# Rational layer: numerators of a couple in one PSUM tile, and another split of the ratio between VectorE and GpSimd

## The chip, the cores and the metric

The kernel runs on one core of a Trainium2 chip. The metric is the device time of one launch in microseconds (us); lower is better. Engines are named as in the profile: PE is TensorE, DVE VectorE, ACT ScalarE, POOL GpSimd, SP the queue that issues most DMAs.

## The reference

Four layers run one after the other on x of shape (8, 16, 128, 128). Each normalises x in groups (2 channels to a group), computes a convolution-like function of it, and adds the result to x. Layer 0 is a small attention block over 3x3 patches, layer 1 a gated 1x1 convolution, layer 2 the rational convolution that the change touches, layer 3 a spline convolution. Layer 2 is:

```python
def _L2_conv_ref(x, A, Bc):
    K, DEG_P, DEG_Q = 3, 6, 4
    B, C, H, W = x.shape
    xp = jnp.pad(x, ((0, 0), (0, 0), (1, 1), (1, 1)))
    wins = jnp.stack([xp[:, :, i:i + H, j:j + W] for i in range(K) for j in range(K)])
    pw = wins[..., None] ** jnp.arange(DEG_P, dtype=x.dtype)
    P = jnp.einsum('pbchwi,fcpi->fpbchw', pw, A)
    Q = 1.0 + jnp.abs(jnp.einsum('pbchwi,fcpi->fpbchw', pw[..., 1:1 + DEG_Q], Bc))
    out = jnp.sum(P / Q, axis=(1, 3))
    return jnp.transpose(out, (1, 0, 2, 3))
```

For each of the 9 positions of the window, each input channel c and each output channel f there is one polynomial P of degree 5 and one denominator Q = 1 + |polynomial of degree 4|. The ratios are summed over the positions and the input channels. So 9 x 16 x 16 ratios are made for each of 8 x 128 x 128 pixels, and their number sets the work.

## The kernel before

All of x stays in SBUF, as 128 partitions (8 images x 16 channels) by 16384 pixels. In layer 2 a helper `powers` (line 929) makes x to x^5 of two image rows and sends them to DRAM; `turn` (line 955) loads ten rows of them, with halo, into four of eight tiles `f`, where 32 partitions hold the powers of four channels. The profile shows all 64 calls of `powers` at work between 3546 and 3893 us, near the layer's start, while the first couples run.

The layer's unit of work is a **couple** (class at line 981): for 8 rows from `r0`, a half `g` of the images, a half `k` of the rows (4 rows, 512 pixels), a window position `n`, and two images out of four (`i`). There are 16 x 2 x 2 x 9 x 2 = 1152 couples. A couple has two halves `ab`, one for each image, and each half is a PSUM tile of 128 partitions by 2 banks of 512 columns: 4 channels to a 32-row strip of TensorE, 16 outputs to a channel, so that 256 (channel, output) pairs fill 128 partitions twice. The steps of a couple are:

- `product` (line 966): four matmuls of 32 rows by 64 columns for the denominators `pd` (weights `wb`), four more for the numerators `pn` (weights `wa`), for each half. In the profile an f32 matmul is two records, so a half of `pd` or `pn` is 8 records.
- `absolute` (line 989), ACT: t = |pd|, 1024 columns for each half, into the SBUF tile `t` (4 buffers).
- `ln` and `exp` (lines 994 and 999), ACT, through the helper at line 152: u = ln(1 + t), then u = exp(-u), a first estimate of 1/Q; 2048 columns each, in the SBUF tile `u` (4 buffers).
- `step` (line 1002), DVE: t = (t + 1) u, which is Q times the estimate.
- `times` (line 1008), DVE, one for each half: u = pn u, the ratio before correction.
- The ratio corrected by one Newton step is u (2 - t). It is made in two ways. For the first bank of each half, `ratio` (line 1014, DVE) forms (t - 2) u. For the second bank, `correction` (line 1021, POOL) forms v = t u, and TensorE adds 2 u - v. `correction` waits until the next couple's step has ended (line 1025).
- `over_channels` (line 1046), PE: the sums over 4 channels by matmuls with the constant `gather`, into the accumulators `acc0` and `acc1`, in three parts: part 0 the finished ratios with weight -1, part 1 u with weight 2, part 2 v with weight -1. It serves two couples at a time, 4 matmuls of 512 columns to a part. After the last position the accumulator is added to x, and the statistics for layer 3 are taken (lines 1067 and 1068).

The order on ACT and on DVE is written out by hand: `in_turn` (line 210) ties each instruction of an engine to the one named before it. On PE only the sums are tied, behind the last product issued; the products follow the order in which they are written and what they wait for. The main loop (line 1087) runs over couples `m`; `before` is couple m-1, `then` m+1. Within a turn ACT does absolute(m, half 1), ln(m), absolute(m+1, half 0), exp(m), and DVE does times(m-1, half 1), ratio(m-1), step(m), times(m, half 0). `products` (line 1030) interleaves the numerators of one couple's half with the denominators of another's, matmul by matmul. PSUM has 8 banks: `pd` takes one buffer of 2, `pn` two buffers of 2, and the accumulators 2.

Of the kernel before, what the change touches and what calls it, by code (L numbers as in the profile page):

```python
# [9 lines left out]
F32 = mybir.dt.float32  # L10
AF = mybir.ActivationFunctionType
ALU = mybir.AluOpType
# [5 lines left out]
BC = B * C  # L18
HW = H * W
HP, WP = H + 2, W + 2  # L20
NCH = HW // 512
# [79 lines left out]
def kernel(  # L101
# [20 lines left out]
    nc = tc.nc  # L122
    mm = nc.tensor.matmul
# [3 lines left out]
    cpool = ctx.enter_context(tc.tile_pool(name="const", bufs=1))  # L127
# [15 lines left out]
    order = mybir.DependencyInfo(mybir.DependencyClass.NoSync, mybir.DependencyReason.DATA)  # L143
# [66 lines left out]
    def in_turn(engine, ins):  # L210

        if engine in chain:
            tc.add_manual_dep(ins, chain[engine].name, order, reason="in turn")
        chain[engine] = ins
        return ins
# [3 lines left out]
    for n in range(5):  # L219
        t = cpool.tile([BC, BC], F32, name=f"w1_{n}")  # L220
        nc.gpsimd.memset(t, 0.0)
        for b in range(B):
            r = slice(b * C, (b + 1) * C)
# [7 lines left out]
    bn1 = cpool.tile([BC, NCH, 6], F32, name="bn1")  # L231
    top = cpool.tile([BC, NCH], F32, name="top")
    x1d = dram.tile([BC, HW], F32, name="x1d")
    with ExitStack() as l0:
        wp = l0.enter_context(tc.tile_pool(name="w0", bufs=1))
        with tc.tile_pool(name="x0", bufs=2) as xp:
            bn0 = xp.tile([BC, NCH, 6], F32, name="bn0", bufs=1)
            for j in range(8):
                t = xp.tile([BC, HW // 8], F32, name="xj")
# [3 lines left out]
            mean0, _, rs0, d0 = group_stats(bn0, "0")  # L243
        lo, hi = _WHERE["center"][1], _WHERE["last"][2]
# [24 lines left out]
        for a in range(2):  # L269
            src = aff_d[:, a : a + 1].rearrange("(d p g c) a -> p g c (d a)", p=2, g=2, c=C)  # L270
            for odd in range(2):
                for g in range(2):
                    for i in range(3):
                        r = 64 * (g ^ odd) + 16 * i
# [489 lines left out]
    with ExitStack() as l1:  # L764
# [93 lines left out]
        class Chunk:  # L858
# [10 lines left out]
            def product(self, p, w):  # L869
                for i in range(2):  # L870
                    cols = bass.ts(i, 512)
                    in_turn("pe1", mm(p[:, cols], w, self.y[:, cols], start=True, stop=True).ins)
# [37 lines left out]
                    getattr(chunks[i], do)()  # L910


    bn3 = cpool.tile([BC, NCH, 6], F32, name="bn3")
    with ExitStack() as l2:
        wp = l2.enter_context(tc.tile_pool(name="w2", bufs=1))
        tmp = l2.enter_context(tc.tile_pool(name="tmp2", bufs=1))
# [49 lines left out]
        def product(p, w, g, k, n, q):  # L966

            dh, dw = divmod(n, 3)
            for u in range(4):
# [6 lines left out]
                    stop=True,  # L976
                ).ins

        class Couple:
            def __init__(self, r0, g, k, n, i):
                self.r0, self.g, self.k, self.n, self.i = r0, g, k, n, i
                self.pd, self.pn = {}, {}

            def at(self, ab):
                return self.g, self.k, self.n, 2 * self.i + ab

            def absolute(self, ab):
                if ab == 0:  # L990
                    self.t = tmp.tile([128, 2, 2, 512], F32, name="t", bufs=4)
                in_turn("act", nc.scalar.activation(self.t[:, ab], self.pd.pop(ab), AF.Abs).ins)  # L992

            def ln(self):

# [9 lines left out]
                ).ins  # L1005
                self.stepped = in_turn("dve", ins)

            def times(self, ab):
                ins = nc.vector.tensor_mul(self.u[:, ab], self.pn.pop(ab), self.u[:, ab]).ins  # L1009
                in_turn("dve", ins)  # L1010

            def ratio(self):
                r = self.u[:, :, 0]
                ins = nc.vector.scalar_tensor_tensor(  # L1016
                    r, self.t[:, :, 0], 2.0, r, op0=ALU.subtract, op1=ALU.mult
                ).ins
                in_turn("dve", ins)

            def correction(self, behind):

                self.v = tmp.tile([128, 2, 512], F32, name="v", bufs=3)
                ins = nc.gpsimd.tensor_mul(self.v, self.t[:, :, 1], self.u[:, :, 1]).ins  # L1024
                tc.add_manual_dep(ins, behind.name, apart, reason="shared port")

        apart = mybir.DependencyInfo(mybir.DependencyClass.Sync, mybir.DependencyReason.DATA)
        last = {}

        def products(num, ab, den):  # L1030


            todo = []
            if den:
                den.pd[1 - ab] = ps.tile([128, 2, 512], F32, name="pd")
                todo.append(product(den.pd[1 - ab], wb, *den.at(1 - ab)))
            if num:
                num.pn[ab] = ps.tile([128, 2, 512], F32, name="pn", bufs=2)
                todo.append(product(num.pn[ab], wa, *num.at(ab)))
            for _ in range(4):  # L1040
                for p in todo:
                    last["product"] = next(p)

        accs = {}

        def over_channels(couples, part):

            g, k, n = couples[0].g, couples[0].k, couples[0].n
            first, final = g == 0 and n == 0 and part == 0, g == 1 and n == 8 and part == 2
            if first:  # L1050
                accs[k] = ps.tile([BC, 512], F32, name=f"acc{k}")
            for c in couples:
                for ab in range(2):
                    q = 2 * c.i + ab
                    ins = mm(  # L1055
                        accs[k][32 * q : 32 * q + 32],
                        gather[:, int(part == 1), g],
                        (c.u[:, ab, 0], c.u[:, ab, 1], c.v[:, ab])[part],
                        start=first,
                        stop=final,  # L1060
                        skip_group_check=True,
                    ).ins
                    tc.add_manual_dep(ins, last["product"].name, order, reason="late sums")
            if final:
                j = couples[0].r0 // 4 + k
                cols = bass.ts(j, 512)
                nc.vector.tensor_add(x[:, cols], accs[k], x[:, cols])
                nc.vector.bn_stats(bn3[:, j], x[:, cols])
# [12 lines left out]
        turn(0, 0)  # L1081
        for r in range(10, 16, 2):
            powers(r)
        products(None, 1, couples[0])
        couples[0].absolute(0)
        products(None, 0, couples[0])
        for m in range(count + 4):
            c, before, then = (couples[i] if 0 <= i < count else None for i in (m, m - 1, m + 1))
            if c:
                c.absolute(1)  # L1090
            if c or before:
                products(before, 1, then)
            if m % 2 and m >= 3 and m - 3 < count:
                over_channels(couples[m - 3 : m - 1], 0)
            if m % 2 == 0 and m >= 4 and m - 4 < count:
                over_channels(couples[m - 4 : m - 2], 2)
            if before:
                before.times(1)
                before.ratio()
            if c:  # L1100
                if (c.k, c.n, c.i) == (0, 0, 0):
                    if c.g == 0 and c.r0 + 16 < H:
                        for r in range(c.r0 + 16, c.r0 + 24, 2):
                            powers(r)
                    if c.r0 + 8 * c.g < H:
                        turn(c.r0 + 8 * c.g, 1 - c.g)
                c.ln()
                if then:
                    then.absolute(0)
                products(c, 0, then)  # L1110
            if m % 2 and m >= 3 and m - 3 < count:
                over_channels(couples[m - 3 : m - 1], 1)
            if c:
                c.exp()
                c.step()
            if before:
                before.correction(c.stepped if c else before.stepped)
            if c:
                c.times(0)

    mid.close()

# [350 lines left out]
```

## Time and profile before

| | us |
|---|---|
| median of 3 runs | 11128.91 (11128.83 to 11133.0) |
| profiled execution | 11134.61 |
| its span, first to last instruction | 11132.8 |
| first and last start of `step` (line 1003) | 3586.4 and 10563.1 |
| steps started before 3900 us | 37 of 1152 |
| absolute, ln, exp on ACT, mean of one | 1.015, 1.912, 1.902 |
| POOL product of line 470, 1024 and 1536 columns | 2.370 and 3.092 |
| POOL additions of line 582, 512 columns | 1.180 |
| DVE line 398 (512 columns, PSUM to PSUM) and line 400 (PSUM to SBUF) | 0.700 and 0.691 |

A line of the profile's groups names the source line, the engine, the operation, the tile written and those read, the shapes and the number of instructions; behind the first bar it gives the busy time and the mean of one in ns, behind the second the idle time of that engine just before these instructions and who ended it. A line of the timeline gives start and length in us; `x2` merges two instructions that follow each other, and the length is then that of both. Slices are fortieths of the span, 278 us each, and their digits are the busy share in tenths. Rational work fills slices 14 to 38.

### The profile page before, as it was taken

The numbers are of one execution on the slowest core, as the hardware profiler recorded it, in microseconds if no ns is written. First come the engines' busy times: TensorE is split into PE (matmuls) and PEld (weight loads), VectorE is DVE, ScalarE is ACT, GpSimd is POOL, SyncE is SP. The second block draws the span as 40 slices with busy tenths as digits, with TensorE's granted clock in tenths as the row PEclk, the third lists the DMA queues.
The fourth block names the chain that finished last, engine by engine and source line by source line (L and its number), as shares of the span: only waits on it lengthen the run. The fifth ranks groups of instructions, "written<-read, shape, count | busy, mean of one in ns | idle before, by whom it ended". The sixth has DMA issues, their size and how long they took to land.

```text
span 11132.8 us, 173994 instructions
## 1 busy us (share of the span) xinstructions
PE 8824.5 (79%) x72372; PEld 2092.4 (19%) x72372; DVE 9078.7 (82%) x6829; ACT 8772.0 (79%) x7107; POOL 4922.7 (44%) x2681
## 2 busy tenths in 40 slices
PE   5999999999997677777777777777777777777799
PEld 1222222222222111111111111111111111111122
DVE  3555555555555699999999999999999999999977
ACT  2555555555545699999999999999999999999988
POOL 3555555555553734433343343344344333443421
PEclk8999999999998799999999999999999999999999
DMA  1000000000002300000000000000000000000022
GB/s 48 13 15 13 14 13 15 14 13 13 15 6 79 129 15 7 7 13 7 7 10 10 7 7 13 7 7 13 7 7 7 13 7 7 13 7 7 2 61 62
DMA packets 189390, 203.91 MB, mean 18 GB/s; under 512 B 46776, under 2 KB 155448, under 8 KB 186552
## 3 DMA queue, kind: packets, MB, share of 16 engines
q1 hardware_dynamic: 179944, 190.68, 6.2%
q8 instruction: 569, 9.32, 0.3%
q10 hardware_dynamic: 8656, 2.11, 0.1%
q14 instruction: 221, 1.81, 0.1%
HBM read 107.15 MB, written 60.04 MB: 15 GB/s over the span
## 4 chain that ended last, share of the span: by engine, by line
DVE 45%; PE 31%; ACT 14%; issue 5%; POOL 2%; DMA 1%; SPq 1%; DVEq 0%; ACTq 0%; POOLq 0%
DVE t L1003 22%; PE banks L360 18%; DVE u L1009 14%; PE pn L971 10%; ACT t L992 9%; DVE y L518 2%; PE acc L1322 1%; POOL y L527 1%; DVE x L538 1%; PE pd L971 1%; ACT hid L152 1%; ACT u L152 1%; DMA yd<-y 1%; DVE x L630 1%; DVE p L1162 1%
## 5 line engine op out<-in xcount | busy, mean ns | idle before, releaser
L971 PE MATMUL pn<-f,wa 32*64 32x512 f32 x18432 | 3419.6, 625 | 1711.3 <-DVE u L1009 1668.7
L1024 POOL TENSOR_TENSOR v<-t,u 128x1024 f32<-128x1024 f32 x1152 | 2738.1, 2377 | 4020.4 <-DVE t L1003 3860.0
L1009 DVE TENSOR_TENSOR u<-pn,u 128x1024 f32<-128x1024 f32 x2304 | 2715.5, 1220 | 117.7
L971 PE MATMUL pd<-f,wb 32*64 32x512 f32 x18432 | 2600.7, 626 | 157.0 <-ACT t L992 91.7
L1003 DVE SCALAR_TENSOR_TENSOR t<-t,u 128x2048 f32<-128x2048 f32 x1152 | 2631.3, 2284 | 34.2 <-ACT u L152 34.0
L992 ACT ACTIVATE t<-pd 128x1024 f32<-128x1024 f32 x2304 | 2338.2, 1015 | 313.8 <-PE pn L971 307.1
L152 ACT ACTIVATE u<-t 128x2048 f32<-128x2048 f32 x1152 | 2202.9, 1912 | 53.0 <-PE acc L1055 17.4
L152 ACT ACTIVATE u<-u 128x2048 f32<-128x2048 f32 x1152 | 2190.8, 1902 | 0.0
L971 PEld LDWEIGHTS pn<-f,wa 32*64 32x64 f32 x18432 | 751.0, 131 | 3774.7 <-DVE u L1009 3246.5
L1016 DVE SCALAR_TENSOR_TENSOR u<-t,u 128x1024 f32<-128x1024 f32 x1152 | 1420.1, 1233 | 37.6
L152 ACT ACTIVATE hid<-banks 128x1024 f32<-128x1024 f32 x576 | 571.8, 1023 | 1049.9 <-PE banks L360 1048.1
L527 POOL TENSOR_TENSOR y<-y 128x1536 f32<-128x1536 f32 x256 | 894.6, 3494 | 834.4 <-DVE y L518 834.4
L1055 PE MATMUL acc<-u,const 128*32 128x512 f32 x9216 | 1257.4, 618 | 1.9 <-DVE u L1016 1.9
L518 DVE TENSOR_TENSOR y<-banks,vp 128x1536 f32<-128x1536 f32 x384 | 673.2, 1753 | 274.7 <-PE banks L360 271.6
L544 ACT ACTIVATE sq<-x 128x1024 f32<-128x1024 f32 x384 | 398.0, 1054 | 412.4 <-DVE x L538 289.8
L470 POOL TENSOR_TENSOR pd<-q,kp 128x1536 f32<-128x1536 f32 (+1 forms) x256 | 693.4, 2731 | 8.0 <-PE banks L360 6.3
L971 PEld LDWEIGHTS pd<-f,wb 32*64 32x64 f32 x18432 | 514.6, 132 | 753.5 <-ACT t L992 691.9
L360 PE MATMUL banks<-att,const 32*128 32x512 f32 x2304 | 498.8, 668 | 173.7 <-DVE att L509 95.9
L360 PE MATMUL banks<-h,wfc 64*128 64x512 f32 (+1 forms) x3072 | 620.8, 633 | 14.5 <-DVE h L606 14.5
L1055 PE MATMUL acc<-v,const 128*32 128x512 f32 x4608 | 616.5, 606 | 0.2 <-POOL v L1024 0.2
L606 DVE TENSOR_TENSOR h<-banks,x 128x1024 f32<-128x1024 f32 x192 | 232.5, 1211 | 438.0 <-ACT hid L152 227.6
L360 PE MATMUL banks<-rstd,const 32*128 32x512 f32 (+1 forms) x1216 | 411.5, 641 | 19.4 <-DVE rstd L400 15.1
(181 smaller groups left out, 7337.0 us busy)
## 6 DMA issues: line engine op xcount, KB each, us to landing
f<-yd SPq DMA_DIRECT2D x512, 101.6 KB
yd<-y SPq DMA_DIRECT2D x320, 130.0 KB
xin<-in_x SPq DMA_DIRECT2D x752, 32.0 KB
four<-sil SPq DMA_DIRECT2D x256, 65.0 KB
xj<-in_x SPq DMA_DIRECT2D x8, 1024.0 KB
xl<-in_x SPq DMA_DIRECT2D x32, 256.0 KB
x1d<-xl SPq DMA_DIRECT2D x32, 256.0 KB
x<-x1d SPq DMA_DIRECT2D x8, 1024.0 KB
```

The costliest lines, as they stand in the source:

```text
L152: ins = nc.scalar.activation(out_, in_, func, **kw).ins
L360: in_turn("pe", mm(*args, skip_group_check=True, **kw).ins)
L470: ins = nc.gpsimd.tensor_mul(t[:, :n].rearrange("p n (a b) -> p n a b", a=4), rows(self.q[d][:, k]).unsqueeze(1).to_broadcast([128, n, 4, W]),
L518: ins = nc.vector.tensor_mul(y.rearrange("p n (a b) -> p n a b", a=4), banks[:, 1:4].rearrange("p n (a b) -> p n a b", a=4), windows(v, j, 3),
L527: in_turn("pool", nc.gpsimd.tensor_add(self.y[k], self.y[k], y).ins)
L971: yield mm(p[64 * (u % 2) : 64 * (u % 2) + 64, u // 2], w[lo : lo + 32, q % 2, n].rearrange("p c f -> p (c f)"), fs[g * NP + q][lo : lo + ...
L992: in_turn("act", nc.scalar.activation(self.t[:, ab], self.pd.pop(ab), AF.Abs).ins)
L1003: ins = nc.vector.scalar_tensor_tensor(self.t, self.t, 1.0, self.u, op0=ALU.add, op1=ALU.mult).ins
L1009: ins = nc.vector.tensor_mul(self.u[:, ab], self.pn.pop(ab), self.u[:, ab]).ins
L1016: ins = nc.vector.scalar_tensor_tensor(r, self.t[:, :, 0], 2.0, r, op0=ALU.subtract, op1=ALU.mult).ins
L1024: ins = nc.gpsimd.tensor_mul(self.v, self.t[:, :, 1], self.u[:, :, 1]).ins
L1055: ins = mm(accs[k][32 * q : 32 * q + 32], gather[:, int(part == 1), g], (c.u[:, ab, 0], c.u[:, ab, 1], c.v[:, ab])[part], start=first, sto ...
```

## The change

Both numerators of a couple now lie in one PSUM tile `pn` of 4 banks, with a single buffer; they are made together, 8 matmuls in a row (`numerators`). The denominators are made by themselves, half by half (`denominators`), in one buffer of 2 banks as before. The split between DVE and POOL moves from 512 and 512 columns of a half to 384 and 640 (`NR`), and it now runs across the two banks of a half, which `flat` joins to 1024 columns. `times` is two instructions for the couple in place of one for each half: the first takes columns 0 to 384 of both halves and writes its result over the numerators in PSUM; the second takes columns 384 to 1024 and writes u. `ratio` reads the first product from PSUM and writes u. `correction` takes 640 columns of each half.

`over_channels` sums part 0 as 384 columns, and parts 1 and 2 in two pieces of 512 and 128 columns each. Part 1 now comes first and opens the accumulator. All matmuls of the layer are tied in one order, `pe2`. The loop looks further ahead: in turn m, exp and step are those of couple m, ln is that of m+1, absolute and the second denominators are those of m+2, and the first denominators those of m+3. The statistics for layer 3 use layer 1's buffer (`bn3 = bn1`), and `v` grows from 512 to 640 columns (3 buffers).

```diff
-    bn3 = cpool.tile([BC, NCH, 6], F32, name="bn3")
+    bn3 = bn1
...
+        NR = 384
+
+        def flat(t):
+            return t.rearrange("p a b c -> p a (b c)")
...
+            def denominators(self, ab):
+                self.pd = ps.tile([128, 2, 512], F32, name="pd")
+                for ins in product(self.pd, wb, *self.at(ab)):
+                    in_turn("pe2", ins)
+
+            def numerators(self):
+
+                self.pn = ps.tile([128, 2, 2, 512], F32, name="pn")
+                both = [product(self.pn[:, ab], wa, *self.at(ab)) for ab in range(2)]
+                for _ in range(4):
+                    for p in both:
+                        in_turn("pe2", next(p))
...
-            def times(self, ab):
-                ins = nc.vector.tensor_mul(self.u[:, ab], self.pn.pop(ab), self.u[:, ab]).ins
-                in_turn("dve", ins)
...
+            def times(self):
+                for cols in (slice(0, NR), slice(NR, 1024)):
+                    p, u = flat(self.pn)[:, :, cols], flat(self.u)[:, :, cols]
+                    in_turn("dve", nc.vector.tensor_mul(u if cols.start else p, p, u).ins)
 
             def ratio(self):
-                r = self.u[:, :, 0]
+                t, p, u = (flat(a)[:, :, :NR] for a in (self.t, self.pn, self.u))
                 ins = nc.vector.scalar_tensor_tensor(
-                    r, self.t[:, :, 0], 2.0, r, op0=ALU.subtract, op1=ALU.mult
+                    u, t, 2.0, p, op0=ALU.subtract, op1=ALU.mult
                 ).ins
                 in_turn("dve", ins)
 
             def correction(self, behind):
 
-                self.v = tmp.tile([128, 2, 512], F32, name="v", bufs=3)
-                ins = nc.gpsimd.tensor_mul(self.v, self.t[:, :, 1], self.u[:, :, 1]).ins
+                self.v = tmp.tile([128, 2, 1024 - NR], F32, name="v", bufs=3)
+                t, u = (flat(a)[:, :, NR:] for a in (self.t, self.u))
+                ins = nc.gpsimd.tensor_mul(self.v, t, u).ins
                 tc.add_manual_dep(ins, behind.name, apart, reason="shared port")
...
-            first, final = g == 0 and n == 0 and part == 0, g == 1 and n == 8 and part == 2
+            first, final = g == 0 and n == 0 and part == 1, g == 1 and n == 8 and part == 2
...
+            pieces = [(512, 1024), (NR, 512)] if part else [(0, NR)]
+            for i, (lo, hi) in enumerate(pieces):
+                for c in couples:
+                    for ab in range(2):
+                        q = 2 * c.i + ab
+                        src = c.v[:, ab, lo - NR : hi - NR] if part == 2 else None
+                        ins = mm(
+                            accs[k][32 * q : 32 * q + 32, lo % 512 : (hi - 1) % 512 + 1],
+                            gather[:, int(part == 1), g],
+                            flat(c.u)[:, ab, lo:hi] if src is None else src,
+                            start=first and i == 0,
+                            stop=final and i == 1,
+                            skip_group_check=True,
+                        ).ins
+                        in_turn("pe2", ins)
...
+        for c in couples[:2]:
+            for ab in range(2):
+                c.denominators(ab)
+                c.absolute(ab)
+            if c is couples[0]:
+                c.ln()
+        couples[2].denominators(0)
+        for m in range(count + 2):
+            before, c, then, far, next_ = (
+                couples[i] if 0 <= i < count else None for i in range(m - 1, m + 4)
+            )
             if c:
...
                 c.exp()
                 c.step()
+                c.numerators()
+            if far:
+                far.absolute(0)
+                far.denominators(1)
+            if then:
+                then.ln()
+            if m % 2:
+                if m >= 3:
+                    over_channels(couples[m - 3 : m - 1], 2)
+            elif 2 <= m <= count:
+                over_channels(couples[m - 2 : m], 1)
+                over_channels(couples[m - 2 : m], 0)
+            if far:
+                far.absolute(1)
+            if next_:
+                next_.denominators(0)
             if before:
                 before.correction(c.stepped if c else before.stepped)
             if c:
-                c.times(0)
+                c.times()
+                c.ratio()
```

More of the change, by code (lines that the diff above doesn't have):

```diff
@@ L983, in __init__ @@
                 self.r0, self.g, self.k, self.n, self.i = r0, g, k, n, i
-                self.pd, self.pn = {}, {}
             def at(self, ab):
                 return self.g, self.k, self.n, 2 * self.i + ab
+            def denominators(self, ab):
[8 more added lines that the diff above has]
+                        in_turn("pe2", next(p))
             def absolute(self, ab):
@@ L991, in absolute @@
                     self.t = tmp.tile([128, 2, 2, 512], F32, name="t", bufs=4)
-                in_turn("act", nc.scalar.activation(self.t[:, ab], self.pd.pop(ab), AF.Abs).ins)
+                in_turn("act", nc.scalar.activation(self.t[:, ab], self.pd, AF.Abs).ins)
             def ln(self):
@@ L1021, in correction @@
             def correction(self, behind):
-                self.v = tmp.tile([128, 2, 512], F32, name="v", bufs=3)
-                ins = nc.gpsimd.tensor_mul(self.v, self.t[:, :, 1], self.u[:, :, 1]).ins
+                self.v = tmp.tile([128, 2, 1024 - NR], F32, name="v", bufs=3)
+                t, u = (flat(a)[:, :, NR:] for a in (self.t, self.u))
+                ins = nc.gpsimd.tensor_mul(self.v, t, u).ins
                 tc.add_manual_dep(ins, behind.name, apart, reason="shared port")
         apart = mybir.DependencyInfo(mybir.DependencyClass.Sync, mybir.DependencyReason.DATA)
[L1028 to L1042, printed above, removed]
         accs = {}
@@ L1048, in over_channels @@
             g, k, n = couples[0].g, couples[0].k, couples[0].n
-            first, final = g == 0 and n == 0 and part == 0, g == 1 and n == 8 and part == 2
+            first, final = g == 0 and n == 0 and part == 1, g == 1 and n == 8 and part == 2
             if first:
                 accs[k] = ps.tile([BC, 512], F32, name=f"acc{k}")
[L1052 to L1063, printed above, removed]
+            pieces = [(512, 1024), (NR, 512)] if part else [(0, NR)]
[13 more added lines that the diff above has]
+                        in_turn("pe2", ins)
             if final:
@@ L1083 @@
             powers(r)
[L1084 to L1099, printed above, removed]
+        for c in couples[:2]:
[9 more added lines that the diff above has]
+            )
             if c:
@@ L1106 @@
                         turn(c.r0 + 8 * c.g, 1 - c.g)
[L1107 to L1113, printed above, removed]
                 c.exp()
                 c.step()
+                c.numerators()
[14 more added lines that the diff above has]
+                next_.denominators(0)
             if before:
```

## The prediction

> **What bounds the kernel now.** I read the page's busy time and slices first, to find which engine is full and where. The rational layer is slices 14 to 38:
>
> ```profile
> span 11132.8 us, 173994 instructions
> PE 8824.5 (79%) x72372; PEld 2092.4 (19%) x72372; DVE 9078.7 (82%) x6829; ACT 8772.0 (79%) x7107; POOL 4922.7 (44%) x2681
> ...
> DVE  3555555555555699999999999999999999999977
> ACT  2555555555545699999999999999999999999988
> POOL 3555555555553734433343343344344333443421
> ```
>
> 82% and 79% are averages over layers; inside this layer VectorE (DVE) and ScalarE (ACT) both read 9. The table of stretches separates them:
>
> ```profile
> core 0: us, PE busy (x) PEld busy (x) DVE busy (x) ACT busy (x) POOL busy (x), PEclk, DMA share, GB/s
> 6000.00:8000.00 2000.00, 1476.74 (x14776) 302.10 (x14768) 1952.88 (x1362) 1894.31 (x1344) 795.88 (x337) 0.99 0.04 9
> ```
>
> DVE is busy 97.6%, ACT 94.7%. A couple costs 4 ACT instructions, so 336 couples pass in 2000 us: 5.952 us each. The groups give the prices:
>
> ```profile
> L1024 POOL TENSOR_TENSOR v<-t,u 128x1024 f32<-128x1024 f32 x1152 | 2738.1, 2377 | 4020.4 <-DVE t L1003 3860.0
> L1009 DVE TENSOR_TENSOR u<-pn,u 128x1024 f32<-128x1024 f32 x2304 | 2715.5, 1220 | 117.7
> L1003 DVE SCALAR_TENSOR_TENSOR t<-t,u 128x2048 f32<-128x2048 f32 x1152 | 2631.3, 2284 | 34.2 <-ACT u L152 34.0
> L992 ACT ACTIVATE t<-pd 128x1024 f32<-128x1024 f32 x2304 | 2338.2, 1015 | 313.8 <-PE pn L971 307.1
> L1016 DVE SCALAR_TENSOR_TENSOR u<-t,u 128x1024 f32<-128x1024 f32 x1152 | 1420.1, 1233 | 37.6
> ```
>
> What matters is from start to start, in the order of time on DVE:
>
> ```profile
> 6001.26 2.28 DVE L1003 SCALAR_TENSOR_TENSOR t<-t,u 128x2048 f32<-128x2048 f32 x1
> 6003.65 2.35 DVE L1009 TENSOR_TENSOR u<-pn,u 128x1024 f32<-128x1024 f32 x2
> 6006.04 1.22 DVE L1016 SCALAR_TENSOR_TENSOR u<-t,u 128x1024 f32<-128x1024 f32 x1
> 6007.18 2.28 DVE L1003 SCALAR_TENSOR_TENSOR t<-t,u 128x2048 f32<-128x2048 f32 x1
> ```
>
> The period is 5.92 us (7.18 - 1.26) and DVE does not rest in it. Where an instruction does not need the one in front, it starts before that one's end: 1.14 from ratio to the next step, though ratio lasts 1.22. Step to times (times overwrites what step reads) takes 2.39, 0.18 more than 2.28 - 0.08. Layer 3's alternating pair of 1024 columns shows the same two distances, 1.14 and 1.32. The mean of 5.952 has 0.03 more than 5.92 from the residual sums (lines 1067 and 1068), which stay. ACT in the same order:
>
> ```profile
> 6001.27 1.91 ACT L152 ACTIVATE u<-t 128x2048 f32<-128x2048 f32 x1
> 6003.09 1.00 ACT L992 ACTIVATE t<-pd 128x1024 f32<-128x1024 f32 x1
> 6003.99 1.90 ACT L152 ACTIVATE u<-u 128x2048 f32<-128x2048 f32 x1
> 6006.14 1.02 ACT L992 ACTIVATE t<-pd 128x1024 f32<-128x1024 f32 x1 [0.24 <-PE pn L971]
> ```
>
> Unhindered, ACT passes a logarithm or exponential in 1.82 and an absolute in 0.90: 5.44 a couple. It waits for PE, but has 1.3 us in hand: the exponential ends at 6005.89, the step that reads it starts at 6007.18. So DVE is the bound, and ACT stands only 0.5 us behind it. PE:
>
> ```profile
> 6007.21 0.66 PE L971 MATMUL pd<-f,wb 32*64 32x512 f32 x4
> 6007.69 0.61 PE L971 MATMUL pd<-f,wb 32*64 32x512 f32 x4
> 6008.24 1.07 PE L1055 MATMUL acc<-u,const 128*32 128x512 f32 x8
> ```
>
> A lone set of denominators (4 matmuls, 8 records) holds PE for 1.03 (7.21 to 8.24); a full set of 8, from 6010.85 to 6011.90, for 1.05; a sum over channels, from 6000.06 to 6001.05, for 0.99.
>
> **The change, part by part.**
>
> **DVE.** One couple had 2048 (step) + 1024 + 1024 (times) + 1024 (ratio) = 5120 columns. It will have 2048 + 768 + 1280 + 768 = 4864. From 1220 ns at 1024 and 2284 at 2048 a column costs 1.04 ns, and 1.14 from start to start leaves 0.07 fixed. No instruction of the new order needs the one directly in front: times' first part writes pn, which step does not touch; its second part and ratio take other columns; the next step is another couple's. So: step 2.21, times 0.87 and 1.41, ratio 0.87, together 5.36. If the first and second times, which share a bank, and the second times and ratio are nevertheless held in order, each adds 0.18: 5.72. Below: nothing under 5.36. The first times now writes PSUM. Line 398 writes PSUM in 700 ns for 512 columns, its twin at line 400 writes SBUF in 691: nothing. Ratio now reads PSUM: 1220 (times, PSUM) against 1233 (ratio, SBUF), nothing again.
>
> **GpSimd (POOL)** goes from 512 to 640 columns of each half: 2.37 x 1.25 = 2.96. It starts 0.15 behind step's end (6003.69 against 6003.54). Ends: 2.73, between the 2370 (1024 columns) and 3092 (1536) of line 470; 3.16, by the 2.53 that v took at 3659.82 beside other work. I take 2.96. It is covered by times and ratio, 3.15 in all. Without that cover it meets a step with two SBUF inputs; at 3674.79 the ratio with such inputs took 1.75 instead of 1.23 beside a POOL product of 0.73, so a meeting costs up to 0.5.
>
> **The order of ACT** becomes exponential, absolute, logarithm (of the next couple), absolute. No neighbours depend on each other: 5.44.
>
> **A new loop.** t has four buffers. absolute(m+2) needs the one that correction(m-2) reads, and that correction waits for step(m-1). So: step 2.28, 0.15, correction 2.96, about 0.1 to ACT, then 0.90 + 1.82 + 0.90 + 1.90 to the end of exponential(m+1), about 0.1 to step(m+1): 11.11 us for two couples, **5.56 each**. (The 0.1 lies between the 0.06 from DVE to PE at 6004.93 and POOL's 0.15.) With the bounds of the correction: 5.44 to 5.66.
>
> **PE.** One pn of four banks replaces two of two: numerators(m+1) wait for ratio(m), the last reader. They start 0.14 into the next step and take 1.05; step lasts 2.28, so about 1.1 us of cover is left; without it times would wait on them. Behind the waiting numerators PE holds, in strict order, denominators(m+2), sums, denominators(m+3), and ACT waits for both denominators. An even turn has 1.05 + 1.03 + 0.99 + the piece of 128 columns + the piece of 384 (0.74) + 1.03. No piece of 128 is in the trace: by columns it costs 0.25, by records as much as a whole one, 0.99; 0.45 taken, nearer the first, since the 8 weight loads go out within 0.16. Even turn 5.29 (5.09 with 0.25; 6.08 with 0.99 for both short pieces), odd turn 4.55. A new loop again: numerators 0.14 in, 5.29, 0.1 to absolute, 5.52 to the exponential's end, 0.1 to step two couples on: 11.15, or 5.57, level with the other.
>
> **The rest.** Shared statistics buffer (bn3 is bn1): read last in layer 1, nothing. DMA issues are the same; turn's loads still come 33 couples before their first reader, some 180 us, and no queue gets more. The start and the drain differ by a few microseconds. The first 37 couples, before 3900 us, run in step with the powers (8 us a couple there): no gain from them, at worst 37 x 0.59 = 22 us lost to the longer correction.
>
> **The sum.** 5.56 + 0.03 = 5.59 against 5.952: 0.362 x 1115 couples = 404 us. The profiled execution took 11134.6 (span 11132.8, 1.8 around it): 10731. It lies 5.7 above the median of the runs, so **10725**.
>
> **Rivals.** Each time is 11128.9 less (5.952 - period - 0.03) x 1115.
> 1. *DVE stays the bound* at 5.72, because times and ratio are held in order. For it: step to times paid 0.18 in every couple. Against it: different columns; ratio's own strided halves cost nothing. Time 10904. A like case is no overlap at all between instructions, which costs the sum of the durations: 2.28 + 0.95 + 1.49 + 0.96 = 5.68, or 10860. Against it stands the 1.14 behind a ratio of 1.22 in every couple. The Trainium skill (VectorE: DVE Perf Modes, The DRAIN you can't avoid) states this case as the rule: the next instruction does not start until the pipe is empty, unless it is one that is not held; the trace agrees with the exception, by that 1.14.
> 2. *The loops don't bind*: a correction of 2.73 and short pieces at 0.25, so ACT's own 5.44 does. For it: line 470. Against: v's own row is linear with the smaller POOL products (1.18 at 512). Time 10592.
> 3. *PE's queue becomes the bound, and it is slower.* The even loop is 5.86 plus the even turn, for two couples; from a turn of 5.98 on it is no faster than before. With both short pieces at 0.99 the turn is 6.08, the period 5.97, the time 11182. For it: a narrow matmul has as many records and weight loads as a wide one; two changes of the array's shape per turn. Against: PE is busy 74% now, and 8 weight loads went out in 0.16.
>
> **How the numbers follow.** Forecast (periods of 5.50 to 5.66, 10658 to 10837) 0.62; rival 1 0.13, of which 0.02 for no overlap; rival 2 0.10; rival 3 0.10; 0.05 for something between rivals 1 and 3, 0.03 of that within 0.2% of before. 0.2% is about what a measurement of this kernel can tell from no change. Faster 0.87, same 0.03, slower 0.10. The range is 10580 to 10950: all of the forecast, rivals 1 and 2, not 3.
>
> **What would show it.** Period in 6000 to 8000 us near 5.59, so some 358 couples; DVE busy share below 97%, with small waits of step on the exponential; absolute waiting for POOL (the t loop) or PE (the queue); correction at 2.96; times 0.95 and 1.49, ratio 0.95; the start distance of the two times 0.87 (free) or 1.05 (held). It is wrong if times waits for PE's numerators, or if the correction outlasts ratio and step stretches beyond 2.28.

## The result, and the profile after

The changed kernel takes 10726.33 us, the median of 5 runs (10723.83 to 10731.1), against 11128.91: a ratio of 0.9639 with a 95% interval of 0.9627 to 0.9652. The profiled execution took 10728.63 us with a span of 10726.8. The forecast was 10725.

The page after, busy time and slices:

```profile
span 10726.8 us, 191623 instructions
PE 9016.0 (84%) x81588; PEld 2440.6 (23%) x81588; DVE 8720.1 (81%) x6829; ACT 8613.6 (80%) x7107; POOL 5545.4 (52%) x2681
...
DVE  3555555555555569999999999999999999999977
ACT  2555555555554679999999999999999999999988
```

The table of stretches after (2000 us of the steady part):

```profile
core 0: us, PE busy (x) PEld busy (x) DVE busy (x) ACT busy (x) POOL busy (x), PEclk, DMA share, GB/s
6000.00:8000.00 2000.00, 1650.86 (x18689) 432.80 (x18681) 1979.98 (x1457) 1976.53 (x1438) 1051.19 (x359) 1.00 0.04 10
```

ACT now passes 1438 / 4 = 359.5 couples where it passed 336, or 5.56 us a couple. DVE and ACT are both 99% busy, and PE rose from 74% to 83%: three engines are nearly full. The groups that answer to those shown before:

```profile
L1043 POOL TENSOR_TENSOR v<-t,u 128x1280 f32<-128x1280 f32 x1152 | 3374.3, 2929 | 2990.1 <-DVE t L1020 2960.8
...
L1009 ACT ACTIVATE t<-pd 128x1024 f32<-128x1024 f32 x2304 | 2348.6, 1019 | 86.6 <-POOL v L1043 42.3
...
L1030 DVE TENSOR_TENSOR u<-pn,u 128x1280 f32<-128x1280 f32 x1152 | 1718.1, 1491 | 39.4
...
L1030 DVE TENSOR_TENSOR pn<-pn,u 128x768 f32<-128x768 f32 x1152 | 1104.2, 959 | 0.0
L1034 DVE SCALAR_TENSOR_TENSOR u<-t,pn 128x768 f32<-128x768 f32 x1152 | 1087.6, 944 | 0.0
```

Line 1009 is `absolute`, and what ends the largest part of its idle time (42.3 of 86.6 us) is no longer PE but POOL's correction. Idle times this small hide the mechanism; it shows in the order of time. DVE after (start, length, line):

```profile
6004.71 2.29 DVE L1020 SCALAR_TENSOR_TENSOR t<-t,u 128x2048 f32<-128x2048 f32 x1
6006.92 0.96 DVE L1030 TENSOR_TENSOR pn<-pn,u 128x768 f32<-128x768 f32 x1
6007.91 1.49 DVE L1030 TENSOR_TENSOR u<-pn,u 128x1280 f32<-128x1280 f32 x1
6009.32 0.94 DVE L1034 SCALAR_TENSOR_TENSOR u<-t,pn 128x768 f32<-128x768 f32 x1
6010.26 2.29 DVE L1020 SCALAR_TENSOR_TENSOR t<-t,u 128x2048 f32<-128x2048 f32 x1
...
6015.74 2.29 DVE L1020 SCALAR_TENSOR_TENSOR t<-t,u 128x2048 f32<-128x2048 f32 x1
```

POOL and ACT in the same couples:

```profile
6007.14 2.93 POOL L1043 TENSOR_TENSOR v<-t,u 128x1280 f32<-128x1280 f32 x1 [2.56 <-DVE t L1020]
```

```profile
6010.10 1.02 ACT L1009 ACTIVATE t<-pd 128x1024 f32<-128x1024 f32 x1
6011.02 1.90 ACT L152 ACTIVATE u<-t 128x2048 f32<-128x2048 f32 x1
6012.82 1.01 ACT L1009 ACTIVATE t<-pd 128x1024 f32<-128x1024 f32 x1
6013.73 1.91 ACT L152 ACTIVATE u<-u 128x2048 f32<-128x2048 f32 x1
```

Read the three together: the step of 6004.71 ends at 7.00, the correction behind it runs from 7.14 to 10.07, absolute starts at 10.10, the exponential ends at 15.64, and the step two couples on starts at 15.74. That is the loop of the prediction: 11.03 us for two couples, 5.515 each, or 5.566 in the mean of 1078 steps in 6000 us. In the trace this is no single case: behind 1019 of the 1057 corrections that end between 4000 and 9890 us the next absolute starts 0.02 to 0.06 later, 0.03 in the median. DVE alone would be just behind: 2.21 + 0.99 + 1.41, and 0.88 or 0.94 from ratio to step.

### The profile page after: what moved, and what is told of

It is laid out like the page before. It is cut to its first block, busy times and chain, and to the rows that moved or that the text cites. A ratio compares the mean times of both kernels' runs of the same rounds, so it can differ in the third digit from the quotient of the medians.

```text
span 10726.8 us, 191623 instructions
## 1 busy us (share of the span) xinstructions
PE 9016.0 (84%) x81588; PEld 2440.6 (23%) x81588; DVE 8720.1 (81%) x6829; ACT 8613.6 (80%) x7107; POOL 5545.4 (52%) x2681
## 4 chain that ended last, share of the span: by engine, by line
DVE 42%; PE 24%; issue 21%; ACT 7%; POOL 3%; DMA 2%; SPq 1%; ACTq 0%; DVEq 0%; POOLq 0%
PE banks L360 18%; DVE u L1030 15%; DVE pn L1030 10%; DVE u L1034 8%; DVE y L518 2%; DVE t L1020 2%; PE pn L971 2%; PE pd L971 2%; PE acc L1334 1%; POOL y L527 1%; DVE x L538 1%; ACT u L152 1%; DMA yd<-y 1%; ACT hid L152 1%; SPq L1298 1%
## 5 line engine op out<-in xcount | busy, mean ns | idle before, releaser
L1043 POOL TENSOR_TENSOR v<-t,u 128x1280 f32<-128x1280 f32 x1152 | 3374.3, 2929 | 2990.1 <-DVE t L1020 2960.8
L971 PE MATMUL pd<-f,wb 32*64 32x512 f32 x18432 | 2518.4, 610 | 332.8 <-ACT t L1009 301.0
L1009 ACT ACTIVATE t<-pd 128x1024 f32<-128x1024 f32 x2304 | 2348.6, 1019 | 86.6 <-POOL v L1043 42.3
L971 PE MATMUL pn<-f,wa 32*64 32x512 f32 x18432 | 1324.8, 624 | 938.4 <-DVE u L1034 938.1
L1030 DVE TENSOR_TENSOR u<-pn,u 128x1280 f32<-128x1280 f32 x1152 | 1718.1, 1491 | 39.4
L1062 PE MATMUL acc<-u,const 128*32 128x512 f32 (+2 forms) x13824 | 1118.9, 456 | 0.0
L1030 DVE TENSOR_TENSOR pn<-pn,u 128x768 f32<-128x768 f32 x1152 | 1104.2, 959 | 0.0
L1034 DVE SCALAR_TENSOR_TENSOR u<-t,pn 128x768 f32<-128x768 f32 x1152 | 1087.6, 944 | 0.0
L1062 PE MATMUL acc<-v,const 128*32 128x512 f32 (+1 forms) x9216 | 749.9, 443 | 1.5 <-POOL v L1043 1.5
L971 PEld LDWEIGHTS pn<-f,wa 32*64 32x64 f32 x18432 | 279.5, 131 | 1947.3 <-DVE u L1034 1936.7
```

Source lines behind the costliest of these rows:

```text
L971: yield mm(p[64 * (u % 2) : 64 * (u % 2) + 64, u // 2], w[lo : lo + 32, q % 2, n].rearrange("p c f -> p (c f)"), fs[g * NP + q][lo : lo + ...
L1009: in_turn("act", nc.scalar.activation(self.t[:, ab], self.pd, AF.Abs).ins)
L1030: in_turn("dve", nc.vector.tensor_mul(u if cols.start else p, p, u).ins)
L1034: ins = nc.vector.scalar_tensor_tensor(u, t, 2.0, p, op0=ALU.subtract, op1=ALU.mult).ins
L1043: ins = nc.gpsimd.tensor_mul(self.v, t, u).ins
L1062: ins = mm(accs[k][32 * q : 32 * q + 32, lo % 512 : (hi - 1) % 512 + 1], gather[:, int(part == 1), g], flat(c.u)[:, ab, lo:hi] if src is N ...
```

## The experiments

Two theories had to be told apart for the new bound: the loop through POOL's correction, or DVE alone. The rest of the runs price the parts: the new order without the new split, ratio's operand in PSUM, and TensorE's strict order. A split of 320 columns was planned too; with its larger `v` the layer's buffers need 85.7 kb of a partition where 84.3 are free, so there is no time for it, and 336 columns took its place.

| kernel | us, median | ratio to the kernel before, 95% interval | period in us, mean of 4000 to 10000 us (to the last step, 9950, in the last row) |
|---|---|---|---|
| the change | 10726.33 | 0.9639 [0.9627, 0.9652] | 5.566 |
| ratio_sbuf | 11325.79 | 1.0174 [1.0159, 1.0190] | 6.12 |
| split512 | 11072.02 | 0.9946 [0.9929, 0.9962] | 5.90 |
| split512_busy | 10916.95 | 0.9807 [0.9794, 0.9820] | 5.79 |
| sums3 | 11141.28 | 1.0008 [0.9999, 1.0017] | 5.94 |
| split336 | 10846.22 | 0.9742 [0.9726, 0.9759] | 5.66 |
| t6 | 10751.01 | 0.9659 [0.9644, 0.9673] | 5.587 |
| t6w | 10651.94 | 0.9569 [0.9556, 0.9582] | 5.500 |
| t6_368 | 10715.40 | 0.9627 [0.9613, 0.9642] | 5.55 |
| staged | 10623.70 | 0.9545 [0.9531, 0.9560] | 5.618, with the later powers in it |
| t6w_368_staged | 10520.53 | 0.9450 [0.9437, 0.9463] | 5.53, with the later powers in it |

**ratio_sbuf: ratio's operand back in SBUF**

```diff
-  in_turn("dve", nc.vector.tensor_mul(u if cols.start else p, p, u).ins)
+  in_turn("dve", nc.vector.tensor_mul(u, p, u).ins)
...
-  t, p, u = (flat(a)[:, :, :NR] for a in (self.t, self.pn, self.u))
+  t, u = (flat(a)[:, :, :NR] for a in (self.t, self.u))
...
-  u, t, 2.0, p, op0=ALU.subtract, op1=ALU.mult
+  u, t, 2.0, u, op0=ALU.subtract, op1=ALU.mult
```

> Changed kernel, but the first times writes its product into u in SBUF and ratio reads it there, so that ratio has two SBUF inputs, beside the correction on GpSimd, which in the changed kernel is still running for some 0.75 us of ratio's time (correction 7.14 to 10.07, ratio from 9.32 in the couple whose step starts at 4.71). Theory (the two engines hinder each other only where the VectorE instruction has two SBUF inputs): ratio or the correction stretches by about 0.5 us a couple (the 1.75 against 1.23 us seen beside GpSimd in the kernel before), period 5.9 to 6.1 us instead of 5.52, time 11150 to 11350 us. Rival (the place of the operands does not matter, only the number of columns): period 5.4 to 5.55, time 10620 to 10740 us, ratio at 0.95 us.

DVE's and POOL's order of time in this kernel (start, length, line):

```profile
6005.76 2.28 DVE L1020 SCALAR_TENSOR_TENSOR t<-t,u 128x2048 f32<-128x2048 f32 x1
6008.14 2.35 DVE L1030 TENSOR_TENSOR u<-pn,u 128x768 f32<-128x768 f32 x2
6010.41 1.51 DVE L1034 SCALAR_TENSOR_TENSOR u<-t,u 128x768 f32<-128x768 f32 x1
6011.85 2.28 DVE L1020 SCALAR_TENSOR_TENSOR t<-t,u 128x2048 f32<-128x2048 f32 x1
```

```profile
6008.18 2.93 POOL L1043 TENSOR_TENSOR v<-t,u 128x1280 f32<-128x1280 f32 x1 [3.16 <-DVE t L1020]
```

The same 768 columns take 1.51 us instead of 0.94 where both inputs lie in SBUF and the correction is still running (to 6011.11, so 0.70 of overlap); the correction keeps its 2.93. Two SBUF inputs by themselves are not enough: in the kernel before, ratio has them too, starts as the correction ends (6003.69 + 2.37 = 6006.06, ratio from 6006.04) and takes 1.22 for 1024 columns. Step to the first times takes 2.38 again (times overwrites what step reads), and the two times are 0.11 closer: 5.46 (DVE's own sum, shown below under t6w) + 0.57 + 0.17 - 0.11 = 6.09, the distance of the two steps. The time is 11326, on the theory's side, and slower than before the change. So a ratio that reads PSUM is not a detail: with both inputs in SBUF the whole gain of the wider product on POOL is lost. The Trainium skill (GPSIMD Engine Reference, Key points) says that GpSimd shares its SBUF interfaces with VectorE and that the two contend where the VectorE instruction has two SBUF inputs; the trace agrees, 1.51 against 0.94 us beside the same product.

**split512: the new order with the old split** (and the empty piece of the sums left out)

```diff
-  NR = 384
+  NR = 512
```

> Changed kernel with the old split, 512 columns of a half for VectorE's ratio and 512 for GpSimd; everything else (order, PSUM tiles, ratio from PSUM) as changed. VectorE then has its old 5120 columns, and the first and second times lie in different banks. Theory (VectorE passes in order without held pairs): 2.21 + 1.14 + 1.14 + 1.14 = 5.63, or 5.75 if the 0.12 us between the two times of the changed kernel come from something else than the bank they share; time about 10850 to 10980 us; VectorE busy above 99%. The loop through the correction would be down to 5.22 and not bind. Rival (the gain came from the order alone, not from the split): 10726 us. Rival (the gain came from the split alone): 11129 us.

On DVE the couple then takes 2.20 + 1.26 + 1.14 + 1.13 = 5.73 in the undisturbed stretches, inside the forecast of 5.63 to 5.75, but the mean is 5.90 and the time 11072, above the forecast's 10980. The table of stretches shows what was not expected, in the granted clock behind POOL:

```profile
core 0: us, PE busy (x) PEld busy (x) DVE busy (x) ACT busy (x) POOL busy (x), PEclk, DMA share, GB/s
5010.00:5020.00 10.00, 8.49 (x88) 1.78 (x72) 9.93 (x8) 10.00 (x8) 4.63 (x2) 1.00 0.01 2
5020.00:5030.00 10.00, 8.46 (x76) 2.26 (x80) 9.21 (x8) 8.08 (x7) 2.50 (x2) 0.83 0.00 0
```

PE in that stretch:

```profile
5015.46 1.12 PE L971 MATMUL pn<-f,wa 32*64 32x512 f32 x16 [1.03 <-DVE u L1034]
...
5021.20 1.77 PE L971 MATMUL pn<-f,wa 32*64 32x512 f32 x16 [1.50 <-DVE u L1034]
5022.68 2.00 PE L971 MATMUL pd<-f,wb 32*64 32x512 f32 x8
```

The same 16 records took 1.77 instead of 1.12, and the next 8 took 2.00 instead of 1.06. Between 4000 and 10000 us the trace's clock records hold 150 stretches of 3.41 us at half clock, where the kernel before has 30 and the changed one 16. ACT then waits for the denominators and DVE for ACT. I took it for too little work on PE, which stood idle for 1.50 us in front of those numerators, and tested that next.

**split512_busy: more work on PE**

```diff
   pieces = [(512, 1024), (NR, 512)] if part else [(0, NR)]
   pieces = [p for p in pieces if p[0] < p[1]]
+  if part == 2:
+      pieces = pieces * 2
```

> The kernel with the split of 512 and 512, with the sums of part 2 issued twice (v counts double in the result): 8 matmul records, 0.99 us, more on TensorE in each odd turn, where it stood idle for 1.0 to 1.6 us in front of the numerators. Theory (the granted clock fell to half for 3.4 us in every 24 because TensorE had too little to do in some stretch, and the slow matmuls then held up ScalarE and VectorE): the clock stays at 0.99 to 1.00, the period falls from 5.895 to 5.73 with a mean of 5.78, time 10920 to 10970 us, less than 11072 although more work is done. Rival (the clock falls for another reason, such as too much work): no better, 11070 to 11200 us.

With 8 records more in every odd turn the stretches at half clock fall from 150 to 18, and the kernel is 155 us faster, 10917 (forecast 10920 to 10970). More matmuls, less time: too little work on PE was the cause, not too much. So the order alone, with the clock kept up, is worth some 210 us (10917 against 11129), and the split the other 190. The Trainium skill (TensorE: Matmul & The Clock Gate, Part 1) says that the clock falls to half after an idle window of about 3.4 us, with free-running windows; the length of 3.41 us agrees, but PE's longest wait for DVE's ratio in that kernel was 2.2 us, 1.2 on average, so it was never idle for a whole such window and the condition is wider than that wording. The clock records narrow it down: all 150 stretches of split512 begin on one grid of 3.4133 us, to 0.001 us, and in the 3.4 us in front of each PE was busy for 36 to 51% by its records, where it was for 80% in the mean. Another 44 windows of that grid with PE below 52% were not followed by half clock, so these records do not give the exact threshold.

**sums3: more work in the even turns of the changed kernel**

```diff
-  pieces = [(512, 1024), (NR, 512)] if part else [(0, NR)]
+  pieces = [(512, 1024), (NR, 512)] if part else [(0, NR)] * 3
```

> Changed kernel with the sums of part 0 (384 columns, 8 records) issued three times in each even turn, so that these ratios count threefold in the result: 16 records more on TensorE. In the changed kernel the even turn holds TensorE for 0.91 + 0.99 + 1.86 + 1.09 = 4.85 us; here about 6.25. Theory of the prediction's third rival (TensorE's strict order becomes the bound once the even turn is longer than 5.98): period (5.86 + 6.25) / 2 = 6.05, time about 11310 us, slower than before the change. Rival (TensorE has room of its own, the two turns even out: 4.85 + 4.3 us of work in 11.03, and 1.4 more fit): 10720 to 10760 us.

Three engines in the couple where it shows:

```profile
6009.45 2.29 DVE L1020 SCALAR_TENSOR_TENSOR t<-t,u 128x2048 f32<-128x2048 f32 x1 [0.87 <-ACT u L152]
```

```profile
6003.81 1.02 ACT L1009 ACTIVATE t<-pd 128x1024 f32<-128x1024 f32 x1 [0.92 <-PE pd L971]
```

```profile
5999.45 3.22 PE L1062 MATMUL acc<-u,const 128*32 128x512 f32 x40
6002.60 1.09 PE L971 MATMUL pd<-f,wb 32*64 32x512 f32 x8
```

The sums hold PE until 6002.60, the denominators behind them come late, absolute waits 0.92 and step 0.87, in every second couple. The even turn is 4.85 + 1.29 = 6.14; the period is 5.94, against 6.0 by the prediction's formula and 5.52 by the rival, and the time 11141, against 11310 expected and 10720 to 10760 by the rival. So the third rival's mechanism is real, and in size smaller than its formula and than the 6.05 expected. With the change's own 4.85 the formula gives 5.36, below the 5.515 that binds.

**split336: less on VectorE, more on GpSimd** (here and below, the two small buffers that share their place are left out of the cut)

```diff
-  NR = 384
+  NR = 336
```

> Changed kernel with 336 columns of a half for ratio and 688 for GpSimd (two small buffers are shared to make room for the larger v). Theory (the loop correction, absolute two couples on, exponential, step sets the period): correction 2.93 x 688 / 640 = 3.15 us, period 5.52 + 0.22 / 2 = 5.63, mean 5.68, time about 10850 us; absolute waits for GpSimd in every turn by some 0.2 us and step for the exponential. Rival (VectorE is the bound of the changed kernel): 96 columns less on VectorE, 0.10 us less, period 5.39 to 5.45, time 10590 to 10660 us.

ACT and POOL in this kernel:

```profile
6009.60 1.02 ACT L1009 ACTIVATE t<-pd 128x1024 f32<-128x1024 f32 x1 [0.17 <-POOL v L1043]
```

```profile
6006.39 3.18 POOL L1043 TENSOR_TENSOR v<-t,u 128x1376 f32<-128x1376 f32 x1 [2.52 <-DVE t L1020]
```

The correction ends at 6009.57, absolute starts at 9.60. VectorE has 96 columns less and the kernel is 120 us slower: 10846, where the loop said 10850 and VectorE alone 10590 to 10660. This decides for the loop.

**t6 and t6w: the loop cut**

```diff
-  self.t = tmp.tile([128, 2, 2, 512], F32, name="t", bufs=4)
+  self.t = tmp.tile([128, 2, 2, 512], F32, name="t", bufs=6)
...
-  ins = nc.gpsimd.tensor_mul(self.v, t, u).ins
+  ins = nc.gpsimd.tensor_mul(t, t, u).ins
```

> Changed kernel with the correction written over t instead of into v, and six buffers of t instead of four; the same work, but absolute no longer waits for the correction of the couple before last. Theory (the loop through the correction sets the period, VectorE stands right behind it at 2.21 + 0.99 + 1.41 + 0.88 = 5.49): period 5.49 and a mean of 5.53 instead of 5.566, time 10680 to 10700 us, no absolute waits for GpSimd any more, VectorE without gaps. Rival (VectorE alone binds already, the waits of absolute cost nothing): 10726 us.

It missed: 10751, slower than the change. The waits of absolute for POOL are gone, but DVE had become slower by itself. DVE in t6:

```profile
6005.04 0.96 DVE L1030 TENSOR_TENSOR pn<-pn,u 128x768 f32<-128x768 f32 x1
6006.10 1.49 DVE L1030 TENSOR_TENSOR u<-pn,u 128x1280 f32<-128x1280 f32 x1
```

The second times starts 1.07 us behind the first, where the changed kernel has 0.99. With the new buffers it is this instruction, not step, that has to wait for an earlier correction, and it then carries two waits, one of them in a semaphore instruction of its own in front of it. The line's semaphore instructions on DVE's queue in the changed kernel and in t6:

```profile
L1030 DVEq EVENT_SEMAPHORE  x1119: 21/21/21, 3593.3 to 10157.3; - x187
```

```profile
L1030 DVEq EVENT_SEMAPHORE  x2226: 21/21/21, 3591.9 to 10176.8; - x186
```

In t6w the wait is put back on step:

```diff
   self.stepped = in_turn("dve", ins)
+  if done:
+      tc.add_manual_dep(ins, done.corrected.name, apart, reason="u free")
...
-  c.step()
+  c.step(couples[m - 3] if m >= 3 else None)
```

> The kernel with six buffers of t, with step also waiting for the correction of three couples before, so that the second times no longer has to wait for GpSimd itself. With six buffers alone the second times carried two waits and began 1.07 us behind the first instead of 0.99, and VectorE, without a gap, passed in 5.54. Theory (with four buffers the loop through the correction set 5.515; cut, and without that second wait, VectorE's 2.21 + 0.99 + 1.41 + 0.88 = 5.49 is left): period 5.47 to 5.49, some 25 to 45 us less than the changed kernel, 10680 to 10700 us. Rival (the loop cost nothing, VectorE alone set 5.515): 10726 us.

DVE in t6w:

```profile
6007.32 2.28 DVE L1020 SCALAR_TENSOR_TENSOR t<-t,u 128x2048 f32<-128x2048 f32 x1
6009.52 0.96 DVE L1032 TENSOR_TENSOR pn<-pn,u 128x768 f32<-128x768 f32 x1
6010.52 1.49 DVE L1032 TENSOR_TENSOR u<-pn,u 128x1280 f32<-128x1280 f32 x1
6011.92 0.94 DVE L1036 SCALAR_TENSOR_TENSOR u<-t,pn 128x768 f32<-128x768 f32 x1
6012.78 2.28 DVE L1020 SCALAR_TENSOR_TENSOR t<-t,u 128x2048 f32<-128x2048 f32 x1
```

The period is 5.46, every couple alike, and the time 10652, 74 us under the change. The theory holds, and its size was too small: the floor of 5.49 contained a little of the loop's own wait (ratio to step is 0.86 here, 0.88 to 0.94 there). The loop cost 0.055 us a couple, 61 us over 1106 couples. The other 13 us are not shown to be the loop's: the changed kernel has 16 stretches at half clock between 4000 and 10000 us and t6w has one, and what that is worth was not measured apart.

**t6_368** is t6 with 368 columns.

> The kernel with six buffers of t, with 368 columns for ratio instead of 384. Theory (VectorE binds once the loop is cut): 32 columns less on VectorE, period 5.46, correction 3.0 us ending 5.43 behind step's start, just ahead of the next step; time 10640 to 10670 us. Rival (the correction now reaches into the next step, whose two SBUF inputs then hinder it; or ScalarE's 5.44 binds with its small waits): no better than the kernel with 384, 10680 to 10760 us.

10715: 36 us better than t6, so VectorE binds once the loop is cut, but the second wait of the times was still in it, and the forecast of 10640 to 10670 missed for the same reason as t6's.

**staged: the later powers kept out of the first stretch**

```diff
-  for r in range(c.r0 + 16, c.r0 + 24, 2):
-      powers(r)
+  ahead = rows_ahead(range(c.r0 + 16, c.r0 + 24, 2))
...
   tc.add_manual_dep(ins, behind.name, apart, reason="shared port")
+  in_turn("pool2", ins)
...
   c.ratio()
+  if m % 2 and ahead is not None:
+      next(ahead, None)
```

Here `rows_ahead` makes the same powers in steps, tied to the order of DVE and ACT, with both products on DVE; the corrections are tied into one order on POOL with the small fills of the powers' edges.

> Changed kernel with the powers of the later rows tied into the order of the engines, one step of them in every second turn, instead of being brought forward by the scheduler into the stretch from 3546 to 3978 us; their two products move from GpSimd to VectorE. Theory (in that stretch 46 couples take 394 us where 256 would do, because powers and couples wait for each other, so some 140 us are lost there, against 30 for 37 couples in 314 us or some 95 us in the kernel before): the later powers then cost only their own time, 56 x 1.0 us on VectorE, in the steady part, and the time falls by 60 to 110 us to 10620 to 10670 us. Rival (the powers are bound by their DMAs and by the first rows, or cost as much in the steady part as they save): 10700 to 10800 us.

10624, 103 us under the change. By 4000 us 74 steps have been done instead of 46, and the last squares of the powers end at 9010 us instead of 3978. The steady part became slower, 5.618 instead of 5.566, which costs 55 us in 1068 couples, of the 156 us (28 x 5.57) won at the front. Two things changed in that stretch together, and the run does not separate them: between 3600 and 3900 us DVE's busy share is 99% instead of 60 to 65%, and the granted clock 1.00 instead of 0.82 to 0.85.

**t6w_368_staged: all of it together**

> All that helped together: six buffers of t with the wait moved to step, 368 columns for ratio, and the later powers tied into the order. Theory (VectorE binds at 5.46, ScalarE at 5.44 right behind it): from the 10624 us of the staged powers alone some 0.04 to 0.05 us less in each of 1140 couples, 10570 to 10590 us. Rival (ScalarE's waits, now without slack against VectorE, eat the difference): 10600 to 10630 us.

10520.5 us, 0.9450 of the kernel before, below the forecast of 10570 to 10590: this is the fastest kernel found. Staged powers give 103 us and the cut loop 74 on their own, and the 16 columns less of a half gave 36 between t6 and t6_368; together 213, and this run has 206. So the parts nearly add up, and the expected 0.04 to 0.05 us a couple was too little: the steps of this run stand 5.43 apart in the median, those of staged 5.53.

## Why the prediction was right, point by point

**DVE's terms.** Step to times 2.21 (forecast 2.21), times to ratio 1.41 (1.41), ratio to step 0.86 where nothing waits (0.87). The one term missed is between the two times, 0.99 against 0.87: held, as the first rival had it, but for 0.12 instead of 0.18 and in one pair of two. That the bank they share is the cause is not borne out: with 512 columns, in different banks, it was 1.26 against 1.14, the same 0.12. ratio_sbuf, whose first times writes SBUF, has no such gap there.

The semaphores that the trace's records name settle the cause. Semaphore 108 is raised by DVE alone. The second times waits for it, that is, for the end of the first, in the changed kernel, in split512 and in t6w, and starts 0.03 behind that end; in ratio_sbuf it has no such wait and starts 0.08 before that end. The kernel before has the same single wait between times and ratio, and the same gap (1.25 from start to start, where 1.14 is free), though its times writes SBUF; the prediction's merged row `x2` hides it and its text does not count it. So it is a wait that the program sets, and not the write to PSUM; why the program sets it for columns that the first times does not touch is not shown. The prediction's 0.18 comes from step to times in the kernel before, where the wait for 108 is a second one beside that for PE, in a semaphore instruction of its own, and times starts 0.10 behind step's end; the second times of t6 is the same case. The first rival's price was therefore that of two waits.

**The loop** was forecast at 5.56 and is 5.515: correction 2.93 (2.96), the way from POOL to ACT 0.03 (0.1). The mean adds 0.05 to it where the forecast added 0.03. It binds, as said; split336 and t6w show it from both sides.

**PE.** An even turn and the sums of an odd one, in the changed kernel:

```profile
6006.74 1.28 PE L1062 MATMUL acc<-v,const 128*32 128x512 f32 x16
...
6010.32 1.12 PE L971 MATMUL pn<-f,wa 32*64 32x512 f32 x16 [0.82 <-DVE u L1034]
6011.23 1.06 PE L971 MATMUL pd<-f,wb 32*64 32x512 f32 x8
6012.22 1.93 PE L1062 MATMUL acc<-u,const 128*32 128x512 f32 x24
6014.08 1.09 PE L971 MATMUL pd<-f,wb 32*64 32x512 f32 x8
```

The even turn is 0.91 + 0.99 + 1.86 + 1.09 = 4.85, below the forecast's 5.29 and below its lower bound of 5.09: a piece of 128 columns costs 0.29 (1.28 for 16 records, less 0.99) where 0.45 was taken, 384 columns 0.58 (1.86 less 1.28; 0.65 in sums3) instead of 0.74, and the numerators 0.91 instead of 1.05. So the cost of these short matmuls goes nearer by their columns than by their number: 0.29 and 0.58 against 0.99 for 512 columns, with 8 records each. The two loops are therefore not level; the one through PE, (5.86 + 4.85) / 2 = 5.36, has some 0.16 us a couple in hand.

**The step that failed** is the one on the powers. The sum put them at nothing, with "at worst 37 x 0.59 = 22 us lost to the longer correction" in the couples before 3900 us. Only 33 steps had started by then in the kernel before (37 comes from adding windows up, and a step that runs over a window's edge stands in both), and 33 in the changed kernel: nothing was lost there. But the stretch of the powers got 85 us longer (last squares at 3978 instead of 3893), and DVE waits longer in it for POOL's second product of the powers. That this product stands behind the longer corrections on POOL is likely, and was not tested. In the kernel before, 3540 to 3900 us, and in the changed kernel, 3540 to 4000 us:

```profile
DVE y L934 <- POOL y L945: 97.3, 60, 3.7
```

```profile
DVE y L934 <- POOL y L945: 165.2, 60, 14.3
```

By 4000 us 46 steps had started instead of 50, and the 47th comes 24 us later than before, counted from the first. That the forecast time was met to 2 us is luck to that extent: the steady gain was 0.387 us a couple instead of 0.362, some 28 us more over 1105 couples, and the stretch took 24 of them back. That this loss is near the 22 us of the worst case is luck as well, since it did not come where the prediction had it.

**What would have shown it.** The count of couples was right (358 forecast, 359.5 found). The DVE share "below 97%" was wrong, 99%: a loop that binds by 0.055 us leaves hardly a gap.

## What to carry to other kernels

When one engine is relieved, look for the loop that closes over several engines through a buffer: add up its durations and hand-overs, divide by the number of turns it spans, and compare that with each engine's own sum. A bound of this kind showed here as a start that follows the same end by 0.03 us nearly every time, and hardly as idle time, and it can be proved by making the supposed bottleneck lighter and the loop longer at once. And measure the stretch that the average leaves out: at the start of the layer the first 46 couples took 419 us (3584 to 4003) where 46 x 5.566 = 256 would do, and those 163 us are more than the loop cost. (The expectation of staged has 394 us, to the last squares of the powers; its 46 steps had started by 4000 us.)

## What the runs showed of the hardware that was not expected

TensorE's clock can fall to half for 3.41 us in a kernel whose matmuls are 80% busy: 150 times in 6000 us in split512, 30 times in the kernel before and 16 in the changed one. 0.99 us of useless matmuls in every second couple made that kernel 1.4% faster (10917 against 11072). The stretches begin on a grid of 3.4133 us, behind 3.4 us in which PE was busy for 36 to 51% in split512; the exact threshold was not found.

Two instructions of VectorE that follow each other had three distances in these traces. Without a wait on the one in front, the second started 0.08 us before its end (ratio to step in the kernel before, and the two times of ratio_sbuf). With one wait for that end, it started 0.03 behind it (times to ratio before, the two times of the changed kernel). With that wait in a semaphore instruction of its own, because the second waits for another engine too, it started 0.10 behind it (step to times before, the two times of t6). The third case moved the second times of t6 by 0.07 us in every couple (1.07 against 0.99); putting the other wait on step, where it cost nothing, brought it back.
